# Layer 1's shared expert: its first half issued ahead of the routing, in PSUM banks of its own

## The chip, the cores and the metric

The kernel runs on one core of one Trainium2 chip. The metric is the time of one execution on the device in microseconds (us). Engines are called as in the profile: PE is TensorE (matmuls; PEld its weight loads), DVE is VectorE, ACT is ScalarE, POOL is GpSimd, SP is SyncE, which here only starts DMAs. Times within the execution are counted from the start of its span.

## The reference

The reference is a decoder of four layers in fp32; each layer has an attention, a cross attention and a feed-forward part, each added to its input and followed by a layer norm. The input is 8 x 256 tokens of 256 features. The change is in the feed-forward part of layer 1, a mixture of 32 experts with 4 per token, at most 256 tokens per expert, and a shared expert that every token passes:

```
topk_w, topk_idx = top_k(softmax(x @ gate_w.T), 4)     # weights normed to a sum of 1
buf[e, slot] = x[token]                                # slot: place of the token in expert e
gu = einsum('ech,ehi->eci', buf, w_gate_up)
expert_out = einsum('eci,eih->ech', silu(g) * u, w_down)
routed[token] += expert_out[e, slot] * weight
shared = (silu(x @ sg) * (x @ su)) @ shared_w_down     # sg, su: halves of shared_w_gate_up
out = routed + shared
```

## The kernel before, in words

The whole decoder is one program. Tokens lie in SBUF as `X` (16 tiles of 128 tokens) and transposed as `xT` (two tiles of 128 features by 2048 tokens). The program is written in Tile: the text states operations and the tiles they use, a scheduler places them into one instruction queue per engine when the kernel is built, and semaphores join the queues. So the order of a queue is fixed in the built program but is not the order of the text; independent pieces of work are woven into each other. An engine runs its queue in order and stands still while its next instruction waits.

`l1_ffn` (from L1200) has these steps:

- **Loads.** `sgu` (L1210, 256 KB, gate and up weights of the shared expert) and `sd` (L1212, 128 KB, its down weights) into the pool `keep`. The tokens' rows were stored to DRAM (`xd`, L750) by the cross attention before, which also leaves each token's four best experts in `top1` and `top1_i` (L756 to L760, ending in DVE's FIND_INDEX8).
- **Routing** (`route1`). DVE compares the experts' numbers with an iota (`oh`, L1111), sums what each token tile has (`before`, L1126); ACT scales `own` (L1129, 16 instructions) and takes an exp for the gate weights (L1183); PE counts earlier tokens (`pos`, L1133 and L1134, 32 matmuls); ACT casts the result (`pos_bf`, L1136); DVE turns it into places (L1138 to L1146) and `away` (L1148). Then come 16 rounds, one for each token tile: DVE makes three of the four one-hot tiles `at` (L1154), ACT makes the fourth from `off` (L1157, L1158), and PE multiplies each into `found` (L1160); `at` has 4 buffers. `turned` (L1192) are small transpositions among them. The end is ACT's `base` (L1165) and DVE's `take` (L1167), the list of token rows for each half of each expert.
- **The shared expert's first half.** Eight groups of 256 tokens: PE multiplies gate and up into a bank `ph` (through the helper `mm`, L134), ACT takes the silu (L1096, which needs an activation table that an ACT_TABLE_LOAD brings), DVE multiplies it with the up half into `shT` (L1097). `ph` has two banks, so a group waits for the multiply two groups before it.
- **The expert loop**, 32 times: SP loads `we` (L1236, 384 KB, three buffers). POOL gathers two sets of 128 token rows `xe` (L953, three buffers) with indices from `take`; PE transposes them (`pt`, L968), ACT copies (`xeT`, L970). PE multiplies gate and up (`ph`), ACT and DVE make `hT` (silu and multiply, L1096 and L1097), PE multiplies down (`py`), DVE copies (`y`, L1253) and SP stores (L1254). After every fourth expert PE multiplies two tiles of `shT` with `sd`, and DVE adds them to `X` (L1261).
- **Preparation of the next part** (`prepare_l2_xattn`, L1835, and helpers from L1760): DVE makes ternary weights (`low` L1814, L1816) and quantized activations, with POOL's reductions `ctx_all`, `vis_all`, `img_all` (L1768). It depends on little of the above and is woven into the expert loop.

In the built program before, the eight groups stand on PE behind the last `found` and in front of the first expert: the pool of `ph` (`f1p`) is opened when the routing's pool (`f1r`) is closed, and takes its banks.

Of the kernel before, what the change touches and what calls it, by code (L numbers as in the profile page):

```python
# [11 lines left out]
F32 = mybir.dt.float32  # L12
# [6 lines left out]
PSUM = bass.MemoryType.PSUM  # L19

P = 128
B, S, D = 8, 256, 256
NT = B * S // P
NTOK = B * S
# [18 lines left out]
class Net:  # L43
# [1156 lines left out]
    def l1_ffn(self, w):  # L1200
        nc, tc = self.nc, self.tc
        E, K, C = 32, 4, 256
        DROP = E * C
        with (
            tc.tile_pool(name="f1", bufs=1) as keep,
            tc.tile_pool(name="f1w", bufs=3) as work,
            ExitStack() as ctx,
        ):
            sgu = keep.tile([P, 2, 256], F32, name="sgu")
            nc.sync.dma_start(sgu, self.ins["l1f_sgu"].rearrange("p (c n) -> p c n", c=2))  # L1210
            sd = keep.tile([P, D], F32, name="sd")
            nc.sync.dma_start(sd, self.ins["l1f_sd"])  # L1212
            xd, yd = self.xd1, self.yd1
            nc.gpsimd.partition_all_reduce(self.w_scale, self.w_sums[:, : len(L2X)], P, bass_isa.ReduceOp.add)
            with (
                tc.tile_pool(name="f1q", bufs=1) as pool,
                tc.tile_pool(name="f1r", bufs=1, space=PSUM) as ps,
            ):
                take = self.route1(E, K, C, pool, work, ps, keep)
            pool = ctx.enter_context(tc.tile_pool(name="f1l", bufs=1))  # L1220
            none = pool.tile([1, D], F32, name="none")
            nc.vector.memset(none, 0.0)
            nc.scalar.dma_start(yd[DROP : DROP + 1, :], none)
            with tc.tile_pool(name="f1p", bufs=2, space=PSUM) as ps:
                shT = pool.tile([P, NTOK], F32, name="shT")
                for o in range(0, NTOK, 256):
                    ph = ps.tile([P, 2, 256], F32, name="ph")
                    for m in range(2):
                        self.mm(
                            ph[:, m, :],  # L1230
                            [(sgu[:, c, m * P : (m + 1) * P], self.xT[:, c, o : o + 256]) for c in range(2)],
                        )
                    self.silu_mul(shT[:, o : o + 256], ph[:, 0, :], ph[:, 1, :], [P, 256], work)
                for e in range(E):
                    we = work.tile([P, 3 * D], F32, name="we")
                    nc.sync.dma_start(we, self.ins["l1f_experts"][e * P : (e + 1) * P, :])  # L1236
                    wgu = we[:, : 2 * D].rearrange("p (c f) -> p c f", c=2)
                    wd = we[:, 2 * D :]
                    xeT = [self.gathered_T(xd, take[:, 2 * e + n : 2 * e + n + 1], work) for n in range(2)]
                    ph = ps.tile([P, 2, 256], F32, name="ph")  # L1240
                    for m in range(2):
                        for n in range(2):
                            self.mm(
                                ph[:, m, n * P : (n + 1) * P],
                                [(wgu[:, c, m * P : (m + 1) * P], xeT[n][:, c, :]) for c in range(2)],
                            )
                    hT = work.tile([P, 256], F32, name="hT")
                    self.silu_mul(hT, ph[:, 0, :], ph[:, 1, :], [P, 256], work)
                    py = ps.tile([P, 2, D], F32, name="py")
                    for n in range(2):  # L1250
                        self.mm(py[:, n, :], [(hT[:, n * P : (n + 1) * P], wd)])
                    y = work.tile([P, 2, D], F32, name="y")
                    nc.vector.tensor_copy(y, py)  # L1253
                    nc.sync.dma_start(yd[e * C : (e + 1) * C, :].rearrange("(t p) d -> p t d", p=P), y)  # L1254
                    if e % 4 == 3:
                        t = e // 4 * 2
                        po = ps.tile([P, 2, D], F32, name="py")
                        for j in range(2):
                            self.mm(po[:, j, :], [(shT[:, (t + j) * P : (t + j + 1) * P], sd)])
                        x = self.X[:, t : t + 2, :]  # L1260
                        nc.vector.tensor_tensor(x, po, x, ALU.add)  # L1261
                with tc.tile_pool(name="x2a", bufs=2, space=PSUM) as ps2:
                    self.prepare_l2_xattn(pool, ps2)
# [918 lines left out]
```

## Time and profile before

| What | us |
|---|---|
| three runs | 2705.01, 2708.56, 2714.05 (median 2708.56) |
| the profiled execution | 2698.26 |
| its span, first to last instruction | 2696.5 |
| PE, DVE, ACT, POOL busy in the span | 2157.2, 1624.2, 987.7, 935.2 |
| routing: end of the last L756 copy to `take` | 929.5 to 959.5 |
| shared groups on PE | 959.5 to 976.9 |
| expert loop, from its first `ph` | 976.9 to about 1108.5 |

The mean granted PE clock of the span is 0.886 of full speed; it is 0.50 in the whole routing and 1.00 from 962.7 on through the loop. A row of a timeline reads: start, duration, engine, source line, operation, result <- operands, shapes, number of instructions, and in brackets the idle time before it with what ended it. A row of windows gives, for a stretch of the span, the busy time of each engine with its number of instructions, the granted PE clock, the busy share of the DMA engines and GB/s. In the chain that ended last each row is the time that one piece of work or one wait gave to the path that sets the end.

### The profile page before, as it was taken

How to read it: one execution, taken by the hardware profiler on the slowest of the kernel's cores; microseconds unless marked ns; L12 is line 12 of the kernel's file. 1: busy time of each engine (PE TensorE's matmuls, PEld its weight loads, DVE VectorE, ACT ScalarE, POOL GpSimd, SP SyncE). 2: the span in 40 equal slices, each digit the busy share in tenths (PEclk: the TensorE clock that was granted, in tenths of full speed). 3: DMA queues.
4: the chain of work that ended last, by engine and by line, in shares of the span. 5: the costliest groups of instructions: out<-in, count | busy, mean ns of one | idle time of the engine just before them, and what ended most of it. 6: DMA issues, size and time to landing. Idle time of an engine off the chain costs nothing.

```text
span 2696.5 us, 41126 instructions
## 1 busy us (share of the span) xinstructions
PE 2157.2 (80%) x14463; PEld 1564.6 (58%) x14463; DVE 1624.2 (60%) x5567; ACT 987.7 (37%) x2234; POOL 935.2 (35%) x980
## 2 busy tenths in 40 slices
PE   8988789699988688667976777778788778777796
PEld 5656678455565477334544355556667656565575
DVE  4764200566667575246667886758667676654675
ACT  2322233233433332123432343344435434343563
POOL 1021221311111134443110145665566555662122
PEclk9998799799988689778997888889889989887899
DMA  2002431200010137411010021111111111120000
GB/s 83 2 1 65 174 128 56 71 1 1 1 67 17 49 111 228 121 56 32 1 50 10 1 66 44 42 49 44 41 43 42 47 43 41 51 72 16 0 13 20
DMA packets 84173, 135.05 MB, mean 50 GB/s; under 512 B 33445, under 2 KB 53045, under 8 KB 82048
## 3 DMA queue, kind: packets, MB, share of 16 engines
q0 software_dynamic: 52288, 79.27, 10.0%
q1 hardware_dynamic: 28924, 49.45, 5.5%
q10 hardware_dynamic: 2756, 3.72, 0.4%
q8 instruction: 115, 1.88, 0.3%
q14 instruction: 90, 0.74, 0.1%
HBM read 242.90 MB, written 17.70 MB: 97 GB/s over the span
## 4 chain that ended last, share of the span: by engine, by line
PE 36%; DVE 22%; issue 10%; POOL 5%; ACT 4%; DMA 3%; another core or an unknown queue 3%; POOLq 0%; ACTq 0%; DVEq 0%
PE po L1498 5%; PE pp L134 4%; PE sc L134 4%; PE s L134 4%; DVE low L515 2%; DMA xe<-xd,take 2%; PE ph L134 2%; PE sc L482 2%; PE pt L134 2%; DVE low L499 2%; PE sc L603 2%; DVE junk L1446 1%; POOL rows L953 1%; DVE X L189 1%
## 5 line engine op out<-in xcount | busy, mean ns | idle before, releaser
L953 POOL DMA_INDIRECT rows<-in_l2f_table_dram,index x512 | 532.3, 1040 | 337.7 <-issue 121.5
L1498 PE MATMUL po<-rows,diag 128*128 128x256 f32 x768 | 231.8, 440 | 105.1 <-ACT diag L1497 68.1
L1446 DVE SCALAR_TENSOR_TENSOR junk<-rows,X 128x256 f32<-128x256 f32 x512 | 214.8, 420 | 53.4 <-DMA rows<-in_l2f_table_dram,index 32.4
L1498 PEld LDWEIGHTS po<-rows,diag 128*128 128x128 f32 x768 | 155.5, 216 | 156.4 <-ACT diag L1497 82.4
L134 PE MATMUL pp<-xT,w 128*128 128x256 f32 (+1 forms) x672 | 199.5, 436 | 30.6 <-issue 20.4
L134 PE MATMUL ph<-xeT,we 128*128 128x128 f32 x1248 | 182.1, 289 | 19.4 <-DMA we<-in_l0f_experts_dram,wrow 15.0
L590 POOL TENSOR_TENSOR aT<-sides,inv 128x256 f32<-128x256 f32 x64 | 46.7, 730 | 425.8 <-DVE sides L588 310.8
L134 PEld LDWEIGHTS ph<-xeT,we 128*128 128x128 f32 x1248 | 168.5, 199 | 39.3 <-DMA we<-in_l0f_experts_dram,wrow 16.3
L1497 ACT ACTIVATE diag<-ident,dots 128x128 f32<-128x128 f32 x384 | 134.3, 395 | 117.8 <-PE po L1498 48.1
L134 PEld LDWEIGHTS pp<-xT,w 128*128 128x128 f32 x672 | 139.5, 216 | 61.9 <-issue 25.8
L175 PE MATMUL pt<-ident,X 128*128 128x128 f32 x352 | 75.9, 330 | 107.0 <-DVE X L189 89.1
L953 POOL DMA_INDIRECT xe<-xd,take x87 | 85.0, 977 | 204.1 <-DVE y L1074 77.6
L176 ACT COPY xT<-pt 128x512 f32<-128x512 f32 x88 | 51.6, 586 | 271.6 <-PE pt L175 232.4
L175 PEld LDWEIGHTS pt<-ident,X 128*128 128x128 f32 x352 | 49.9, 164 | 140.3 <-DVE X L189 51.6
L134 PE MATMUL py<-we,hT 128*128 128x256 f32 x496 | 129.0, 384 | 0.9 <-DVE hT L1097 0.9
L1074 DVE TENSOR_TENSOR y<-py,we 128x256 f32<-128x256 f32 x23 | 9.8, 425 | 197.5 <-PE py L134 197.5
L554 ACT ACTIVATE e<-sc 128x512 f32<-128x512 f32 (+1 forms) x154 | 81.4, 602 | 103.0 <-PE sc L482 74.2
L1068 ACT ACTIVATE hT<-ph,we 128x128 f32<-128x128 f32 x184 | 65.7, 367 | 119.5 <-PE ph L134 87.9
L482 PE MATMUL sc<-kv,qv 32*128 32x128 f32 (+2 forms) x1448 | 103.9, 320 | 1.8 <-DVE qv L700 0.6
L189 DVE TENSOR_SCALAR X<-z,ln_mv,rs_y 128x256 f32<-128x256 f32 x176 | 68.3, 431 | 51.5 <-POOL rs_y L145 51.3
L482 PEld LDWEIGHTS sc<-kv,qv 32*128 32x128 f32 x1448 | 80.4, 190 | 31.4 <-issue 26.0
L482 PE MATMUL sc<-qv,kv 32*128 32x128 f32 (+2 forms) x1384 | 97.0, 343 | 0.1
(510 smaller groups left out, 5150.3 us busy)
## 6 DMA issues: line engine op xcount, KB each, us to landing
we<-in_l1f_experts_dram SPq DMA_DIRECT2D x32, 384.0 KB
yd<-y SPq DMA_DIRECT2D x32, 256.0 KB
rows<-in_l2f_table_dram,index POOLq DMA_INDIRECT x512
w<-in_l2x_w_dram SPq DMA_DIRECT2D x1, 4096.0 KB
yd<-y SPq DMA_DIRECT2D x23, 128.0 KB
X<-in_x_dram SPq DMA_DIRECT2D x8, 256.0 KB
xd<-X ACTq DMA_DIRECT2D x8, 256.0 KB
xd<-X SPq DMA_DIRECT2D x8, 256.0 KB
```

The costliest lines, as they stand in the source:

```text
L134: self.nc.tensor.matmul(out, lhsT=lhsT, rhs=rhs, start=n == 0, stop=n == last and bias is None)
L175: nc.tensor.transpose(pt[:, c, j, :], self.X[:, i0 + j * step, c * P : (c + 1) * P], self.ident)
L189: nc.vector.tensor_scalar(self.X[:, i, :], z[:, j, :], mv[:, j, 0:1], r[:, j : j + 1], ALU.subtract, ALU.mult)
L482: nc.tensor.matmul(sc[: shape[0], part], lhsT=lhsT, rhs=rhs, start=mask is None, stop=True, skip_group_check=True)
L499: nc.vector.tensor_reduce(low5[:, r, :, :, 0], sc, AX.X, ALU.max, negate=True)
L515: nc.vector.tensor_reduce(low4[:, r, :, 0], sc, AX.X, ALU.max, negate=True)
L554: lambda r, sc: nc.scalar.activation(e0[m][:n0, r], sc, AF.Exp),
L953: self.nc.gpsimd.indirect_dma_start(out=out, out_offset=None, in_=table, in_offset=bass.IndirectOffsetOnAxis(ap=index, axis=0), **({} if r ...
L1068: nc.scalar.activation(hT[:, g + f, :], ph[:, f, :], AF.Gelu, bias=b1[:, g + f : g + f + 1])
L1446: nc.vector.scalar_tensor_tensor(junk, row, 1.0, self.X[:, i, :], ALU.mult, ALU.mult, accum_out=out)
L1497: nc.scalar.activation(diag, self.ident, AF.Copy, scale=dots[:, k : k + 1])
L1498: nc.tensor.matmul(po, lhsT=diag, rhs=rows[:, k, D:], start=False, stop=g + k == H * K - 2)
```

## The change

The eight groups of the shared expert's first half are written in front of the call of `route1`. Their banks come from a new pool `f1s` (two banks), open beside the routing's pool `f1r`. `shT` moves from the pool opened after the routing to `keep`. The experts' `ph` still comes from `f1p`. Nothing else is changed; the lines below the new text stand two lines further down.

```diff
@@ -1212,25 +1212,27 @@
             nc.gpsimd.partition_all_reduce(self.w_scale, self.w_sums[:, : len(L2X)], P, bass_isa.ReduceOp.add)
+            shT = keep.tile([P, NTOK], F32, name="shT")
             with (
                 tc.tile_pool(name="f1q", bufs=1) as pool,
+                tc.tile_pool(name="f1s", bufs=2, space=PSUM) as ps2,
                 tc.tile_pool(name="f1r", bufs=1, space=PSUM) as ps,
             ):
+
+                for o in range(0, NTOK, 256):
+                    ph = ps2.tile([P, 2, 256], F32, name="ph")
+                    for m in range(2):
+                        self.mm(
+                            ph[:, m, :],
+                            [(sgu[:, c, m * P : (m + 1) * P], self.xT[:, c, o : o + 256]) for c in range(2)],
+                        )
+                    self.silu_mul(shT[:, o : o + 256], ph[:, 0, :], ph[:, 1, :], [P, 256], work)
                 take = self.route1(E, K, C, pool, work, ps, keep)
...
             with tc.tile_pool(name="f1p", bufs=2, space=PSUM) as ps:
-                shT = pool.tile([P, NTOK], F32, name="shT")
-                for o in range(0, NTOK, 256):
-                    ph = ps.tile([P, 2, 256], F32, name="ph")
-                    for m in range(2):
-                        self.mm(
-                            ph[:, m, :],
-                            [(sgu[:, c, m * P : (m + 1) * P], self.xT[:, c, o : o + 256]) for c in range(2)],
-                        )
-                    self.silu_mul(shT[:, o : o + 256], ph[:, 0, :], ph[:, 1, :], [P, 256], work)
                 for e in range(E):
```

## The prediction

> **What bounds the kernel now.** I read the page first, then the table of windows around the shared expert, then the timelines of TensorE (PE), ScalarE (ACT) and VectorE (DVE) there, the chain that ended last, and the waits of the DMA queue.
>
> ```profile
> PE 2157.2 (80%) x14463; PEld 1564.6 (58%) x14463; DVE 1624.2 (60%) x5567; ACT 987.7 (37%) x2234; POOL 935.2 (35%) x980
> ```
>
> PE is the busiest engine, but 80% is a mean over stages. The windows (us; busy PE, PEld, DVE, ACT, POOL; granted PE clock; DMA share; GB/s) cut this stage:
>
> ```profile
> 929.20:933.40 4.20, 0.01 (x1) 0.00 (x0) 3.87 (x18) 0.24 (x2) 0.49 (x1) 0.50 0.46 168
> 933.40:938.70 5.30, 3.29 (x32) 2.04 (x32) 4.92 (x30) 3.41 (x17) 0.00 (x0) 0.50 0.81 264
> 938.70:942.90 4.20, 0.00 (x0) 0.00 (x0) 3.44 (x7) 0.79 (x2) 0.00 (x0) 0.50 0.00 0
> 942.90:959.50 16.60, 11.49 (x160) 8.22 (x160) 11.95 (x55) 14.53 (x34) 0.00 (x0) 0.50 0.00 1
> 959.50:962.70 3.20, 3.15 (x8) 2.53 (x9) 3.10 (x6) 1.28 (x1) 2.61 (x2) 0.50 0.15 41
> 962.70:967.00 4.30, 3.26 (x19) 2.71 (x18) 2.93 (x8) 1.56 (x5) 3.02 (x5) 1.00 0.19 61
> 967.00:976.90 9.90, 9.90 (x47) 8.72 (x46) 8.89 (x20) 2.04 (x6) 1.72 (x2) 1.00 0.15 42
> 976.90:1015.00 38.10, 35.40 (x248) 31.12 (x247) 28.65 (x58) 8.91 (x27) 17.65 (x18) 1.00 0.66 198
> ```
>
> The routing (929.2 to 959.5) is a serial chain through DVE, ACT and PE with PE idle about half the time and at clock 0.50; its longest part is bound by ACT (14.53 of 16.60). Then PE alone works on the shared block until 976.9, and the first expert waits behind it:
>
> ```profile
> 959.54 5.28 PE L134 MATMUL ph<-xT,sgu 128*128 128x256 f32 x16 [0.56 <-DVE take L1167]
> 964.66 0.60 PE L968 MATMUL pt<-ident,xe 128*128 128x128 f32 x4
> 966.55 10.53 PE L134 MATMUL ph<-xT,sgu 128*128 128x256 f32 x48
> 976.91 1.95 PE L134 MATMUL ph<-xeT,we 128*128 128x128 f32 x16
> ```
>
> The chain of waits names what else would have held that expert, and what paces the loop:
>
> ```profile
> 959.79 2.95 DMA xe<-xd,take
> 963.25 2.91 DMA xe<-xd,take
> 986.21 3.50 DMA xe<-xd,take
> 989.86 5.11 DMA xe<-xd,take
> ```
>
> From 977 to 1109 this chain gives 38.7% to these gathers (three `xe` buffers), so the loop is held by gather latency and PE in turn.
>
> **What the change can remove.** With `take` ready at T = 959.49, the third gather lands at 963.25 + 2.91 = T + 6.7; expert 0's `hT` ends at 979.35 + 0.41 = T + 20.3. The built order of the changed kernel puts the first transposition of the third `xe` inside expert 0's `ph`. So there `hT` comes at: T + 6.7 for that landing, + 0.4 transposition, + 12/16 of 1.95 = 1.5 (2.9 at half clock), + silu and multiply 0.4 + 0.4, + hand-overs: T + 9.5 to T + 11. I take T + 10.2, since PE idles before it. The removal is worth 20.3 − 10.2 = 10.1 us if T stays.
>
> **What it adds: T moves.** ACT decides. Before:
>
> ```profile
> 933.37 3.29 ACT L1129 ACTIVATE own<-oh 128x128 bf16<-128x128 bf16 x16 [3.91 <-DVE picks L1182]
> 936.57 0.24 ACT L1183 ACTIVATE picks<-picks 128x64 f32<-128x64 f32 x1
> 938.71 0.58 ACT L1136 CAST pos_bf<-pos 128x512 bf16<-128x512 f32 x1 [1.90 <-PE pos L1134]
> ```
>
> In the changed order ACT runs: 8 of `own`, table load, silu 1 and 2, 8 of `own`, table load, the exp (L1183), table load, silu 3 and 4, `pos_bf`. The load was at 960.21, once, 1.28 us (L1096); now there are three.
> - Entry. `shT` in `keep` shifts the buffers, and the `sgu` load now waits for the last FIND_INDEX8 (L760, ends 930.14), behind which `sd` and the experts' loads queue too. The queue paid that wait before, but for the experts:
>
> ```profile
> SPq L1236 <- DVE w L760: 3.9, 1, 3.9
> ```
>
>   Issued then at 930.28. `sgu` went out at 916.28 and the windows show its traffic over by 918.6 with `sd`: about 2.2 us, so the first group starts at 932.5, not in the gap but inside the routing.
> - Groups 1 and 2 on PE: at 959.54 the first silu came at 963.13 (+3.6), the second at 964.86; the clock rose 3.2 us after the start. Group 2 all at half clock would be +6.9. I take 938.3 for its end.
> - ACT: 933.37 + 1.65 + 1.28 + 0.4 = 936.7 (silu 1); silu 2 waits for group 2: 938.7; `own` 940.3; load 941.6; exp 941.9; load 943.2; silu 3 and 4 943.9 (PE: nineteen `pos` matmuls at 3.29/32 = 0.10 after group 2, then two groups at 1.73, 943.4; multiplies 1 and 2 free their banks before that); PE's last thirteen `pos` matmuls, queued behind group 4, 944.1 at full clock; `pos_bf` ends 944.7. Before: 938.71 + 0.58 = 939.3. That is +5.4.
> - DVE: the multiplies 1 to 4 lie in waits that are there anyway; the fifth (0.42) stands between `half` and `place`. Before, `away` (next fence) ended at 942.66; it moves to 942.66 + 5.4 + 0.42 = 948.5.
>
> ```profile
> 942.49 0.17 DVE L1148 TENSOR_SCALAR away<-place 128x16 f32<-128x16 f32 x1
> 979.35 0.41 DVE L1097 TENSOR_TENSOR hT<-silu,ph 128x256 f32<-128x256 f32 x1
> ```
>
> - Groups 5 to 8 stand on PE in front of the first `found`: 1.73 each at full clock (spacing of the silus from 968.48 on), four of them from 944.3: 951.2. The block itself issues no DMA. ACT has silu 7 and 8 (0.35 each) between `off` and `at`. So the second round's `at` ends at 952.2, 7.2 later than 944.96; `turned` at full clock gives back some 0.4. The rounds after it keep their 0.94, since ACT's `off` and `at` (0.51 + 0.41) set it. T moves by 6.8, to 966.3.
>
> **Sum.** `hT` of expert 0 ends at 966.3 + 10.2 = 976.5 instead of 979.76: −3.3. The loop after it: in the changed order DVE has the same ternary-weight work (L1814, L1816: 0.88 + 1.49 per expert) beside `hT` and `y` (0.41 + 0.69), 3.5 us per expert, which covers the first eight; before, these ran at 3.2 to 4.5 us. The seventh gather, which waited for PE until 979.35, would go out near T + 10.6 = 976.9: −2.4. So the lead of 2 to 4 us lasts; I take −3. Moved or renamed otherwise: `sd` and `we` land long before use; `vis_all` and `img_all` stand behind other gathers on POOL, and DVE's quantized steps wait for them, covered by the loop's 48 us with DVE at 15 busy (1060 to 1108); that costs nothing unless POOL stands waiting. After the loop, the order is the same.
>
> The profiled execution took 2698.26 (span 2696.5, 1.8 around it). 2698.26 − 3 = 2695.3; the median of the runs shown is 10.3 above that execution, so I forecast 2708.56 − 3 = 2705.6. About 0.3% (8.1 us) is what a measurement of this kernel can tell from no change; this is 0.11%.
>
> **Unknown costs, bounded.** The table load: 1.28 us, and at 1162.12 the load was followed by its activation at 1163.42, so nothing more; both ends are that row. The clock: 3.2 us of half clock (959.54) to all of it; the groups cost 1.73 to 3.5 each. The loop: gathers take 2.9 to 5.1 us, so phase alone may move it by ±3 us.
>
> The Trainium skill ("ScalarE: Activation LUTs", What ACT_TABLE_LOAD costs) adds a drain of about 1.38 us to each load of 1.28. By it the three loads ahead of `pos_bf` would cost 4.1 us more and the sum would be +1 instead of −3; the row at 1162.12 shows no such drain, so I do not take it.
>
> The skill ("TensorE: Matmul & The Clock Gate", Part 1) lets the clock rise after a busy window of about 3.4 us that runs free of the program. By it group 2 could end up to 1.6 us later than the row of 959.54 has it, and −3 would become about −2.
>
> **Rivals.**
> - *The routing hides the block* (faster). If ACT's loads and silus fall into its idle time before 938.7 and groups 5 to 8 into DVE's, T moves only by about 3, and `hT` 0 comes at T + 9.5 = 972: −7.8, and −2 for gathers that meet less traffic: −10, 2698.6. For it: ACT is idle 3.9 us before `own`. Against: the order has `own` first, and that waits for `oh`.
> - *PE's queue at half clock* (slower). PE ran at 0.50 through the whole routing, at 62 to 69% busy. If it stays so, groups 3 to 8 take 3.45 instead of 1.73: groups 3 and 4 delay `pos_bf` by 3.4, groups 5 to 8 the first `found` by 6.8 more; expert 0 starts cold, 1.4. With −3: +8.6, 2717.2. It decides from T beyond 969.6, where the lead is gone. Against: PE has 5 us without a gap from 932.5, and the clock rose after 3.2 us of that at 959.54.
> - *The lead is eaten* (no change). The loop is paced by gathers; if its later phase absorbs the lead, 2708.6.
> - That it does not do what it says, with groups starting inside the routing because of `sgu`, is already in the sum.
>
> **How the numbers follow.** Forecast 0.36 (0.02 of it past −0.3%, 0.01 past +0.3%), lead eaten 0.12, hidden 0.29, cold queue 0.23. Faster 0.29 + 0.02 = 0.31; same 0.33 + 0.12 = 0.45; slower 0.23 + 0.01 = 0.24. The forecast's own range is −8 to +3 (loop ±3, clock). The range takes in both rivals' prices and the scatter of the runs shown (±4.5): 2696 to 2718.
>
> **What would show it.** Right: first shared matmul near 932.5; three table loads before 944; `pos_bf` ending 5 us later; `take` near 966; expert 0's `hT` near 976; its `y` waits behind DVE's ternary work. Wrong: `take` before 963 or after 969; granted clock 0.50 through 950; gather waits in the loop much unlike 38.7% of the chain.

## The result, and the profile after

In the same runs on one chip the changed kernel took 2700.06 us (median of 20) and the kernel before 2704.45 (median of 20): a ratio of 0.9983, 95% interval 0.9967 to 0.9999. Repeated on a second chip, the ratio was 1.0001 (0.9986 to 1.0016). Both ratios are nearer to 1 than the 0.3% that a measurement of this kernel can tell from no change; the forecast was 2705.6 against 2708.56, a ratio of 0.9989. The profiled execution after took 2700.39 us with a span of 2698.6.

Executions differ by some us before this stage begins, so all marks below are counted from E, the end of the last FIND_INDEX8 (L760): 930.14 in the profile before, 928.36 after. Lines below the edit are two further down.

The page, and windows that start at the same times as those of the prediction; the stage itself starts 1.8 us earlier here, by E (us; busy PE, PEld, DVE, ACT, POOL; granted clock; DMA share; GB/s):

```profile
PE 2153.4 (80%) x14463; PEld 1564.1 (58%) x14463; DVE 1626.0 (60%) x5567; ACT 990.7 (37%) x2236; POOL 938.8 (35%) x980
```

```profile
933.40:938.70 5.30, 5.30 (x35) 4.30 (x34) 2.33 (x16) 2.40 (x6) 0.00 (x0) 0.66 0.77 268
938.70:942.90 4.20, 3.46 (x28) 2.90 (x26) 2.01 (x11) 4.14 (x10) 0.00 (x0) 1.00 0.01 2
942.90:966.00 23.10, 17.14 (x192) 13.18 (x192) 17.55 (x67) 17.02 (x41) 0.00 (x0) 0.81 0.01 1
966.00:976.90 10.90, 5.73 (x30) 4.87 (x31) 6.83 (x16) 1.67 (x5) 7.28 (x7) 0.61 0.20 61
```

PE's 9.90 of 9.90 in front of the first expert has become 5.73 of 10.90: the block has left that place. PE now fills 933.4 to 938.7 inside the routing, and the routing is longer. TensorE's and ScalarE's timelines there:

```profile
931.36 6.46 PE L134 MATMUL ph<-xT,sgu 128*128 128x256 f32 x16 [3.94 <-DMA sgu<-in_l1f_sgu_dram]
950.61 0.40 PE L1160 MATMUL found<-own,at 128*128 128x64 bf16 x8
```

```profile
933.29 1.28 ACT L1096 ACT_TABLE_LOAD   x1
937.86 0.38 ACT L1096 ACTIVATE silu<-ph 128x256 f32<-128x256 f32 x1 [2.32 <-PE ph L134]
939.85 1.28 ACT L1183 ACT_TABLE_LOAD   x1
941.14 0.26 ACT L1183 ACTIVATE picks<-picks 128x64 f32<-128x64 f32 x1
941.42 1.28 ACT L1096 ACT_TABLE_LOAD   x1
943.25 0.59 ACT L1136 CAST pos_bf<-pos 128x512 bf16<-128x512 f32 x1
```

The first group waits for `sgu` until E + 3.0, silu 2 waits 2.32 us for the second group, three table loads stand ahead of `pos_bf`, and the first `found` comes only at 950.61. On VectorE, `take` and the `hT` of expert 0:

```profile
965.90 0.23 DVE L1167 SCALAR_TENSOR_TENSOR take<-found,base 128x64 uint32<-128x64 f32 x1 [1.35 <-ACT base L1165]
975.77 0.42 DVE L1097 TENSOR_TENSOR hT<-silu,ph 128x256 f32<-128x256 f32 x1 [2.73 <-ACT silu L1096]
```

`take` ends at E + 37.8 (before E + 29.4), the first `hT` at E + 47.8 (before E + 49.6): a lead of 1.8 us where the expert loop starts. At expert 31 nothing of it is left in this pair of profiles: E + 176.4 against E + 176.3.

### The profile page after: what moved, and what is told of

It reads as the page before. It is cut to its first block, busy times and chain, and to the rows that moved or that the text cites. A ratio compares the mean times of both kernels' runs of the same rounds, so it can differ in the third digit from the quotient of the medians.

```text
span 2698.6 us, 41127 instructions
## 1 busy us (share of the span) xinstructions
PE 2153.4 (80%) x14463; PEld 1564.1 (58%) x14463; DVE 1626.0 (60%) x5567; ACT 990.7 (37%) x2236; POOL 938.8 (35%) x980
## 3 DMA queue, kind: packets, MB, share of 16 engines
q0 software_dynamic: 52288, 79.27, 10.1%
## 4 chain that ended last, share of the span: by engine, by line
PE 37%; DVE 21%; issue 9%; POOL 5%; ACT 4%; DMA 3%; another core or an unknown queue 2%; POOLq 0%; ACTq 0%; DVEq 0%; SPq 0%
PE pp L134 5%; PE po L1500 5%; PE s L134 4%; PE sc L134 4%; PE ph L134 2%; DVE low L515 2%; PE sc L482 2%; DVE low L499 2%; PE pt L134 2%; PE s L1646 1%; DMA xe<-xd,take 1%; PE sc L603 1%; POOL w L953 1%; PE pt L175 1%
```

## The experiments

All marks of all profiles, in us after E; ratios are times against the kernel before on the same chip, with 95% intervals. The kernel before itself took 2585 to 2717 us on the chips used, so times are not compared between runs on different chips.

| Kernel | pos_bf | take | hT 0 | hT 31 | ratio |
|---|---|---|---|---|---|
| before | 9.15 | 29.35 | 49.62 | 176.30 | |
| before_2 | 9.15 | 29.34 | 49.52 | 174.72 | 1.0010 (0.9993 to 1.0028) |
| after | 15.48 | 37.77 | 47.83 | 176.40 | 0.9983 (0.9967 to 0.9999) |
| after_2 | 15.49 | 37.77 | 47.86 | 179.60 | 1.0001 (0.9986 to 1.0016) |
| none | 9.15 | 29.34 | 42.69 | 174.30 | 0.9969 (0.9950 to 0.9989) |
| four | 15.47 | 35.66 | 48.32 | 179.58 | 1.0001 (0.9980 to 1.0021) |
| sgu | 13.65 | 34.66 | 45.30 | 180.40 | 0.9984 (0.9965 to 1.0004) |
| sgu4 | 12.42 | 32.59 | 45.81 | 175.22 | one run |
| all4 | 11.94 | 32.14 | 45.60 | 176.89 | 0.9998 (0.9980 to 1.0016) |
| before6 | 9.13 | 29.34 | 49.62 | 168.55 | 0.9975 (0.9962 to 0.9988) |
| before6_2 | 9.19 | 29.39 | 49.68 | 169.22 | 0.9974 (0.9955 to 0.9994) |
| after6 | 15.53 | 37.82 | 48.69 | 170.48 | 0.9960 (0.9946 to 0.9975) |
| all4_6 | 11.92 | 32.13 | 45.57 | 167.23 | 0.9964 (0.9946 to 0.9983) |
| none6 | 9.16 | 29.34 | 41.77 | 164.54 | 0.9929 (0.9904 to 0.9953) |

Up to the first `hT` a mark repeats within 0.1 us, so the routing can be read to a tenth. A whole time cannot: its intervals are 3 to 7 us to each side.

### Without the block (none)

```diff
-                for o in range(0, NTOK, 256):
-                    ...
-                    self.silu_mul(shT[:, o : o + 256], ph[:, 0, :], ph[:, 1, :], [P, 256], work)
+                nc.gpsimd.memset(shT, 0.0)
```

> The kernel before, without the shared expert's first half (eight groups of 8 products, their silus and multiplies); shT is set to zero on GpSimd instead, so the output lacks the gate and up product of the shared expert. All marks are taken from the end E of the last FIND_INDEX8 (L760). Before: take ends at E+29.4, expert 0's hT at E+49.6; changed kernel: E+37.8 and E+47.8. This run is what the change could bring at most: nothing in the routing, nothing in front of expert 0. My theory (the routing is lengthened by the block's own pieces, the removal in front of expert 0 is worth 10): take at E+29.4 (within 0.5), hT at take + 10.1 = E+39.5, and a time 10 us below the kernel before (0.9963), because the lead lasts through the loop. Rival 'the lead is eaten': the same marks, but the last expert's hT moves by less than 4 us and the time falls by less than 4 us (0.9985 or more).

`take` came at E + 29.34 as expected. The first `hT` came at E + 42.7, not E + 39.5: the filler took its share, with 1.80 us on GpSimd in front of the first gather, and VectorE added some 2: the silu had ended at 976.87, but ternary weights stood in VectorE's queue until 978.99, when `hT` began. Of the 6.9 us of lead, 2.0 were left at expert 31 against the first profile of before, 0.4 against the second. That is the rival's mark, a lead that the loop eats. The time itself (0.9969) lies between the two and decides nothing.

### Four groups ahead, four behind (four)

```diff
-                for o in range(0, NTOK, 256):
+                for o in range(0, 4 * 256, 256):
...
             with tc.tile_pool(name="f1p", bufs=2, space=PSUM) as ps:
+                for o in range(4 * 256, NTOK, 256):
+                    ...
```

> The changed kernel with four groups ahead of the routing and four behind take, in the experts' banks. Up to pos_bf the built order is that of the changed kernel. It takes groups 5 to 8 from in front of the first found. Theory 'groups 5 to 8 on TensorE lengthen the routing beyond ScalarE's share': pos_bf ends at E+15.5 as in the changed kernel, take at E+15.5 + 20.2 (the stretch from pos_bf to take of the kernel before) = E+35.7, 2.1 earlier than in the changed kernel; the four late groups hold TensorE for about 8.8 us from take (5.3 for two at the clock that rises 3.2 us after the start, 1.73 each for two more), of which 6.7 lie beside the first three gathers; hT of expert 0 at take + 12.5 = E+48.2, and the time as the changed kernel's, within 2 us. Rival 'ScalarE alone sets it': take stays within 0.5 of E+37.8, hT at E+50, time 2 us above the changed kernel.

Measured: `pos_bf` E + 15.47, `take` E + 35.66, `hT` at take + 12.66 = E + 48.32. With `pos_bf` unmoved, the stretch from there to `take` is 20.19 us, as in the kernel before (20.20), against 22.29 in the changed kernel: groups 5 to 8 in front of `found` cost 2.1 us. TensorE's timeline shows the four late groups:

```profile
963.52 8.95 PE L134 MATMUL ph<-xT,sgu 128*128 128x256 f32 x32 [0.56 <-DVE take L1167]
```

8.95 us, where 8.8 was expected; the saving in the routing is paid back there.

### sgu loaded early (sgu)

```diff
-            shT = keep.tile([P, NTOK], F32, name="shT")
+            shT = ctx.enter_context(tc.tile_pool(name="f1h", bufs=1)).tile([P, NTOK], F32, name="shT")
```

> The changed kernel with shT in a pool of its own behind the work pool, so that the buffer of sgu is the one it had in the kernel before: its load waits only for the attention's last products again and goes out some 12 us earlier. The first group then starts when the gate's last product is through (about E-1) and not at E+3.0. In the built order TensorE then has five groups in front of the pos products and three in front of found. Theory 'sgu's wait is a part of what lengthens the routing': silu 2's wait of 2.32 us goes, pos_bf ends at E+13.3 (12.7 to 14) instead of E+15.5, take at E+35.6 (34.5 to 36.5) instead of E+37.8, hT of expert 0 at E+45.7; time 2 us below the changed kernel. Rival 'the table loads and TensorE's queue set pos_bf whenever the groups start': pos_bf and take within 0.5 of the changed kernel's, the same time.

The first group started at E - 0.64. `pos_bf` at E + 13.65 and `take` at E + 34.66 lie in the ranges given; `hT` of expert 0 came at E + 45.30 (expected 45.7). The placing of `shT` alone, through the buffer that `sgu` got and the order built from it, had cost 1.8 us at `pos_bf`, 3.1 at `take` and 2.5 at the first `hT`. At expert 31 it brought nothing (E + 180.4).

### All three edits (all4), and the table loads alone (sgu4)

```diff
+                picks = pool.tile([P, 2, NT, K], F32, name="picks")
+                ...
+                nc.scalar.activation(picks[:, 1], picks[:, 1], AF.Exp)
                 for o in range(0, 4 * 256, 256):
```

The diff shows the lines of the gate weights that are new in front of the block; the same lines leave `route1`. `shT` and the four late groups are as in the two runs above.

> Three edits of the changed kernel together: sgu's load early (as above), the subtraction and exp of the gate weights issued ahead of the block (so that ScalarE loads its table once ahead of pos_bf, not three times), and four groups ahead of the routing, four behind take. My theory: pos_bf at E+11.4 (11 to 12) against E+9.2 before and E+15.5 in the changed kernel, take at 20.2 more = E+31.6, hT of expert 0 at take + 12.5 = E+44; the time 5.6 us below the kernel before (0.998) and 3.8 below the changed kernel. Rival 'table loads cost nothing, since ScalarE waits anyway': pos_bf no earlier than with the early sgu alone (E+13.3). Rival 'the lead is eaten': marks as in my theory, time within 2 us of the kernel before.

> The changed kernel with sgu's load early and four groups ahead, four behind: the same as the run with all three edits, but with the gate weights' exp where the change leaves it, so ScalarE has three table loads ahead of pos_bf instead of one. Built order on ScalarE: silu 1, own, silu 2, 13 of own, silu 3, 2 of own, load, exp, load, silu 4, pos_bf. Theory 'the two more loads of 1.28 us are on the path': pos_bf ends at E+13.4 against E+11.9 with one load, take at E+33.6 against E+32.1. Rival 'ScalarE waits for TensorE there anyway': pos_bf within 0.4 of E+11.9.

all4: `pos_bf` E + 11.94 (expected 11.4), `take` E + 32.14 (31.6), `hT` E + 45.60 (44), 4.0 us ahead of the kernel before; at expert 31 0.6 behind the first profile of before. Of the 1.6 us that `hT` came late, 0.5 were there at `take`, and 0.8 are the four late groups, which hold TensorE for 9.75 us here and for 8.95 in four. sgu4, with three loads in place of one, had `pos_bf` at E + 12.42: the two loads of 1.28 us cost 0.48, not the 1.5 that I expected and a little more than the rival's 0.4. ScalarE's timeline of all4 shows why:

```profile
932.57 1.28 ACT L1096 ACT_TABLE_LOAD   x1
943.23 0.58 ACT L1136 CAST pos_bf<-pos 128x512 bf16<-128x512 f32 x1 [2.41 <-PE pos L1134]
```

With one load ScalarE waits 2.41 us for TensorE's `pos`; two loads fill that wait first. With the groups early, TensorE's queue sets `pos_bf`, and the loads mostly hide behind it.

### The same pair again, and with six xe buffers

```diff
-        xe = work.tile([P, D], F32, name="xe")
+        xe = work.tile([P, D], F32, name="xe", **({} if bufs is None else dict(bufs=bufs)))
...
-                    xeT = [self.gathered_T(xd, take[:, 2 * e + n : 2 * e + n + 1], work) for n in range(2)]
+                    xeT = [self.gathered_T(xd, take[:, 2 * e + n : 2 * e + n + 1], work, 6) for n in range(2)]
```

> The kernel before, unchanged, for a second profile. E is the end of the last FIND_INDEX8 (L760). In the first profile take ends at E+29.4, hT of expert 0 at E+49.6, of expert 31 at E+176.3. My theory says that these marks repeat within 0.3 up to expert 0 and within 3 at expert 31, where the gathers' landing times scatter. Against the next run it tells whether the lead of 1.8 us of the changed kernel at expert 0 is still there at expert 31.

> The changed kernel, unchanged, for a second profile. In the first one take ends at E+37.8, hT of expert 0 at E+47.8, of expert 31 at E+176.4: a lead of 1.8 us at expert 0 and none at expert 31. Forecast's theory (the lead lasts): in this pair expert 31 is 1 to 4 us earlier than in the kernel before. Rival 'the lead is eaten by the gathers': expert 31 within 1 us of it again, or later, with TensorE's waits for xe in the loop longer than in the kernel before.

> The kernel before with six xe buffers instead of three in the expert loop. Rival 'the loop is paced by gather latency, and eats any lead': TensorE's waits for xe (9.8 us in 980 to 1108 before) nearly go; the stretch from expert 0's hT to expert 31's falls from 126.7 to about 120 to 122 (23 steps of 3.65 and 8 of 4.51 are 120, the steps that TensorE alone sets), and the time falls by 4 to 6 us. Forecast's theory in its plain form (the loop is TensorE's and gathers are hidden): no change over 2 us.

> The changed kernel with six xe buffers. The built order on TensorE is that of the changed kernel through the routing and the first experts. If the gathers eat the lead with three buffers, then with six the loop runs in TensorE's steps from the start in both kernels, and the lead is kept: take at E+37.8, hT of expert 0 at E+47.8, of expert 31 at E+168 to 170, 1.8 us (1 to 3) ahead of the kernel before with six buffers; the time 1.8 us below that kernel's and 6 to 8 below the kernel before. If something else than the gathers eats it, expert 31 comes at the same time in both.

The repeat: lead at expert 0 1.66 us, at expert 31 the changed kernel is 4.88 us behind. The two profiles of one kernel differ by 1.6 (before) and 3.2 us (after) at expert 31: two profiles of each show no lead of either sign that holds at the loop's end with three buffers.

Where the 3.2 us come from can be read in after_2. The steps to its experts 25 and 27 take 6.90 and 6.89 us. TensorE's timeline at the first of them, and the same twelve products one expert later:

```profile
1074.23 0.41 PE L968 MATMUL pt<-ident,xe 128*128 128x128 f32 x2 [2.14 <-DMA xe<-xd,take]
1076.01 2.77 PE L134 MATMUL ph<-xeT,we 128*128 128x128 f32 x12
1081.08 1.50 PE L134 MATMUL ph<-xeT,we 128*128 128x128 f32 x12
```

After a wait of 2.14 us for a gather the granted clock fell from 1.00 to 0.50, from about 1075.6 to 1079, and the twelve products took 2.77 us instead of 1.50; the other step has a wait of 1.97 us and the same fall. From the starts of the rows the two falls cost some 1.6 us each (an estimate). Such steps, of 6.9 to 7.5 us with the clock at 0.50, stand once in four and twice in sgu, behind waits of 1.9 to 2.5 us, and in no other profile between E + 52 and the last `hT`. The length of the wait alone does not decide it: after has a wait of 2.19 us at 1085.35, and its next twelve products took 1.50. What decides it stays open.

TensorE's waits in the loop of before_2, after_2 and before6 (us in total, times, longest):

```profile
PE pt L968 <- DMA xe<-xd,take: 7.6, 8, 1.8
```

```profile
PE pt L968 <- DMA xe<-xd,take: 8.8, 9, 2.1
```

```profile
PE ph L134 <- ACT xeT L970: 5.4, 18, 0.4
PE py L134 <- DVE hT L1097: 0.9, 1, 0.9
```

With six buffers the waits for `xe` are gone, and from expert 16 on the loop runs in steps of 3.65 us, with 4.51 every fourth expert, with hardly an exception. From the first `hT` to the last it took 118.9 and 119.5 us (before6, before6_2) instead of 126.7 and 125.2, a little less than the 120 to 122 expected, and the time fell by 0.25% and 0.26% (some 6.5 and 7 us, where 4 to 6 were expected). So waits for gathers held the loop back by 6 to 8 of its 126 us; the rest is TensorE's own steps.

The last expectation failed in the profile: with the gathers out of the way the lead of after6 did not last either. `hT` in us after E:

| Expert | before6 | after6 | difference |
|---|---|---|---|
| 0 | 49.62 | 48.69 | -0.93 |
| 4 | 64.50 | 64.78 | +0.28 |
| 11 | 91.21 | 91.59 | +0.38 |
| 14 | 103.02 | 104.87 | +1.85 |
| 31 | 168.55 | 170.48 | +1.93 |

The whole times do not show this loss: the medians are 2575.35 us for after6 and 2578.07 for before6, 2.7 the other way, a difference that 12 runs of each do not quite tell from nothing. So what follows is read from the stage's rows alone. About 1.2 us go in experts 1 to 4, nearly all of it in the step from expert 0 to 1 (4.18 us against 3.07). By the rows there are two reasons: in the kernel before, the shared block had let the gathers run ahead, and part of expert 1's products stood in front of expert 0's `hT`; and after6 ran at clock 0.50 until about 976.7, so that four products of expert 1 took 1.21 us instead of 0.71. Another 1.5 go in experts 12 to 14, where one step takes 6.24 instead of 4.51. That same step of 6.24 is in after, after_2 and none6. In the profile after, POOL, DVE and PE there:

```profile
1019.84 0.95 POOL L953 DMA_INDIRECT xe<-xd,take  x1 [1.45 <-PE pt L968]
1021.09 0.94 POOL L953 DMA_INDIRECT xe<-xd,take  x1 [0.30 <-issue]
1022.07 0.31 POOL L1770 PARTITION_ALL_REDUCE vis_all<-vis_m  x1
```

```profile
1017.33 2.15 DVE L1768 TENSOR_REDUCE vis_m<-vis 128x1 f32<-128x1920 f32 x1
1022.41 0.15 DVE L1778 TENSOR_SCALAR vis_step<-vis_all 128x1 f32<-128x1 f32 x1 [2.00 <-issue]
```

```profile
1025.80 0.35 PE L134 MATMUL pp<-q_act,w 128*128 128x448 bf16 x1 [1.28 <-DVE q_act L1793]
```

`vis_m` is ready at 1019.48, but its reduction stands in POOL's queue behind two gathers, the first of which waits for a buffer from PE. DVE then waits 2.00 us and PE, whose queue holds the quantized product in front of the experts' products, 1.28. In the kernel before, POOL met the reduction idle, and waited for it:

```profile
1009.96 0.36 POOL L1768 PARTITION_ALL_REDUCE vis_all<-vis_m  x1 [1.13 <-DVE vis_m L1766]
```

In the built programs this reduction comes after 21 of the loop's gathers before and after 29 in the changed kernel. Every kernel with the block moved or left out shows a wait of DVE for it (1.8 to 2.0 us) and one of PE for `q_act` (1.1 to 1.3 us); none of the profiles of the kernel before shows PE waiting there. An edit that moves this reduction alone was not tried, so its price is read from rows, not shown by taking it away.

### The bound and the best version with six buffers

> The kernel before with six xe buffers and without the shared expert's first half; shT is set to zero on VectorE (in the earlier run without the block GpSimd did it, 1.80 us in front of the first gather). The output lacks the shared expert's gate and up product. It shows what is to be had where the loop runs in TensorE's steps: take at E+29.4; hT of expert 0 at take + 10.1 to 11.0 (10.1 with three buffers, 10.9 with six in the changed kernel) = E+39.5 to 40.4. If a lead lasts in such a loop except for the wait of the quantized products on vis_all, expert 31 comes 119 to 122 later, E+159 to 162, 7 to 9 us ahead of the kernel before with six buffers (E+168.6), and the time falls by as much against that kernel. If something unseen still eats the lead, expert 31 is later than E+165.

> The version that the runs point to: sgu's load early, exp of the gate weights ahead of the block, four groups ahead of the routing and four behind take, and six xe buffers. With three buffers take ended at E+32.1 and hT of expert 0 at E+45.6, 4.0 ahead of the kernel before. Theory 'gathers and the wait on vis_all eat the lead': with six buffers hT of expert 0 at E+45.6 to 46.5, about 1 us lost to the first gathers and 1.1 to 1.7 to TensorE's wait for q_act; expert 31 at E+166 to 167, 2 us ahead of the kernel before with six buffers (E+168.6) and 4 ahead of the changed kernel with six (E+170.5). Rival 'the start does not matter at all': E+168 to 171.

> The kernel before with six xe buffers once more, on the chip of the two runs above: hT of expert 0 at E+49.6, of expert 31 at E+168.6 within 0.5, since no gather's landing time is in the loop's steps any more; time 0.25% below the kernel before.

none6 uses `nc.vector.memset(shT, 0.0)` in place of the block; all4_6 is all4 with the six buffers. none6: `take` E + 29.34, but `hT` E + 41.8, later than the 39.5 to 40.4 expected. Again a reduction in POOL's queue, in its DVE and POOL timelines:

```profile
968.03 0.15 DVE L1769 TENSOR_SCALAR ctx_step<-ctx_all 128x1 f32<-128x1 f32 x1 [4.98 <-issue]
968.96 0.41 DVE L1097 TENSOR_TENSOR hT<-silu,ph 128x256 f32<-128x256 f32 x1
```

```profile
967.67 0.33 POOL L1761 PARTITION_ALL_REDUCE ctx_all<-ctx_m  x1
```

`ctx_all` stands behind eight gathers; DVE waits 4.98 us for it in front of the first `hT`, whose silu had ended at 966.3. Without that, `hT` would have ended near take + 9.8, which fits the 10.1 of the forecast. So the first `hT` is late here for a reason of its own, and the loop starts some 2 us behind what the first gathers alone would allow. At expert 31 none6 is 4.0 to 4.7 us ahead of the two kernels before with six buffers, not 7 to 9 (E + 164.5, between the two marks named). Its time against before6_2 is lower by 0.45 points with an interval of some 0.3 to each side, where the stage shows 0.17; that lies within the interval.

all4_6: `hT` E + 45.57, expert 31 E + 167.23. That is 1.3 and 2.0 us ahead of before6 and before6_2, and 3.3 ahead of after6; in time it is 0.36% (0.17 to 0.54) below the kernel before. So most of what was found comes from the buffers (0.25% and 0.26%); in the profiles the placing of the block adds 1.3 to 2.0 us, in this form. The times do not tell all4_6 (0.9964), after6 (0.9960), before6 and before6_2 (0.9975, 0.9974) apart.

before6_2 repeats before6 within 0.2 us up to expert 22, but at expert 31 it stands at E + 169.22, just outside the 0.5 expected. One step, to expert 23, takes 4.17 us there; none6 and all4_6, on the same chip, have 4.15 and 4.16 at that place, and the two kernels with six buffers on the other chip 3.65. On the same chip, then, all4_6 is 2.0 us ahead of the kernel before with six buffers.

## Why the prediction was right or wrong

The times came out as the case to which the prediction gave the largest chance, no change that can be told (0.45). That is in part luck, since two of its cases give it: a lead of 3 us that lasts, and a lead that the loop eats (0.12). The times do not settle which: −3 lies in both intervals, −8.9 to −0.3 us and −3.6 to +4.1 us, and 0 lies just outside the first and inside the second. The profiles show a lead of 1.8 us where the loop starts, and none at its end. The steps, each from E:

- **sgu.** Right: issued at E + 0.15 (forecast E + 0.14); the first group at E + 3.0 (E + 2.4), and inside the routing.
- **The chain to pos_bf.** Right in kind, low in size: +6.33 instead of +5.4. TensorE stayed longer at half clock: the window 933.40 to 938.70 has a mean of 0.66, which a rise at 937.0 gives, 5.6 us after the first group and not 3.2. So silu 2 ended at E + 9.9 (E + 8.6 by the forecast), within the 1.6 us that the prediction had allowed for a later rise.
- **Groups 5 to 8.** +2.1 from `pos_bf` to `take` (shown by four), 1.4 by the forecast. T moved by 8.4 instead of 6.8.
- **The removal.** `hT` at T + 10.06; the forecast had T + 10.2. That is the term that mattered most, and it held. The lead at expert 0 was 1.8 instead of 3.3, all of the difference being T's. So the sum up to the loop was right in kind and 1.5 us too high.
- **"So the lead of 2 to 4 us lasts; I take −3."** This step failed in the profiles. At expert 31 the changed kernel stands 0.1 and 4.9 us behind with three buffers, 1.3 to 1.9 behind with six. In the first pair with three buffers a lead of 1.0 to 2.9 us held up to expert 20 and was gone at expert 21, after waits of 1.60 and 1.17 us for gathers. In the second, 1.7 us went at expert 12, where `vis_all` is waited for, and more than 4 in the two steps at clock 0.50. The prediction had "phase alone may move it by ±3 us" for the gathers and priced the rest at nothing. Two things of the rest were not nothing. The first steps of the loop cost the changed kernel 0.2 to 0.4 us with three buffers and 1.2 with six; DVE's ternary work beside them did not make them alike. And "that costs nothing unless POOL stands waiting" priced `vis_all` and `img_all` at nothing, while POOL did stand waiting, for buffers from PE: `vis_all` cost about 1.5 us with six buffers. `img_all` did cost nothing; no engine waited for it in after. The rival "the lead is eaten" is the case that the profiles show, though in part by a queue and by a clock that it did not name.
- **Rivals that fell.** The cold queue: the clock was 1.00 from 937.0 to about 957.5, from late in group 2 through group 8, and T came at E + 37.8, which is 967.9 on the scale of the profile before, short of 969.6. Its last part did come: the clock was 0.50 again when expert 0 started, and rose at about 974.5, which T + 10.2 had room for. The hidden block: T moved 8.4, not 3.

The Trainium skill ("ScalarE: Activation LUTs", What ACT_TABLE_LOAD costs) adds a drain of about 1.38 us to a load; here the load at 939.85 ends at 941.13 and the exp starts at 941.14, so the row decides against it.

## What to carry to other kernels

A lead at a loop's start is worth only what the loop lets through: find what paces the loop first, and price that before anything in front of it (here three more gather buffers brought 0.25%, moving a block of 17 us no change that can be told). When work is moved across an in-order queue, look up what changes places on every queue behind it: a reduction of 0.3 us behind two gathers cost about 1.5 us, by the rows of six-buffer loops. And a new tile in an old pool moves the buffers after it, and with them what a load waits for.

## What the runs showed that I had not expected

Once no gather is waited for, the loop repeats to 0.01 us per expert, so a step that differs (6.24 against 4.51, or 4.17 against 3.65 on one chip) names its place at once. With three buffers, two profiles of one program differ by up to 3.2 us over the same loop, and two falls of the clock to 0.50 behind waits of 2 us account for about that much. The granted clock took 5.6 us of products to rise from 0.50 in the profile after, where the profile before had 3.2.
